# Four-layer graph network on one core: values of layers 1 and 2 by seven products, instructions moved off or merged on VectorE, and the first graph's adjacency codes turned by TensorE

## The chip, the core and the metric

The kernel runs on one core of one Trainium2 chip. TensorE (PE) multiplies, VectorE (DVE) and ScalarE (ACT) work element by element, GpSimd (POOL) and SyncE (SP) do little but issue transfers. Each engine works through its own list in order. The metric is the device time of one execution in microseconds (us), the median of several runs; lower is better.

## The reference

32 graphs (B) of 512 nodes (N) with 256 features (H) pass four attention layers, each with a layer norm and a ReLU ahead and a residual sum behind. All values are float32; the adjacency is an int32 matrix of 0 and 1.

```python
# x: (32, 512, 256), adj: (32, 512, 512)
h = relu(layernorm(x))                      # layer 0: two convolutions with one softmax
att = softmax(h @ att_W @ h^T / sqrt(256) + where(adj == 1, 0, -1000))
y = tanh(att @ (h @ W0 + b0)); y = tanh(att @ (y @ W1 + b1))
x = x + y
h = relu(layernorm(x))                      # layer 1
Wh = h @ W^T;  e = leaky(Wh@a1 + (Wh@a2)^T);  x = x + softmax(where(adj > 0, e, -9e15)) @ Wh
h = relu(layernorm(x))                      # layer 2
Hh = h @ W; e = where(adj, exp(-leaky(Hh@s + (Hh@d)^T)), 0); x = x + elu(e @ Hh / rowsum(e))
h = relu(layernorm(x))                      # layer 3
g = h @ W; e = leaky((g@a_1)^T + g@a_2 + g@a_12@g^T)
x = x + elu(h @ W_1 + (softmax(where(adj > 0, e, -9e15)) @ h) @ W_2)
```

## The kernel before

**Tiling.** The graphs are independent. One graph's nodes are four tiles of 128 partitions (NT = 4), its features two chunks of 128 (HC = 2). A matrix of scores is kept turned, as four chunks `e(l, c)` of 128x512 float32. A float32 product stands in the trace as two records of a matmul (a turn by TensorE as one).

**Order of the work.** The function `graph` (L461) writes nothing; it registers operations with an engine, a cost and what they come after. A planner (`Plan`, L53 to L202) then orders all operations of all 32 graphs: a list schedule with due times `APART` and `APART_LAST` (L64) apart, for which it tries several spacings, and margins `SLACK` (L67) on the costs. The instructions are issued in that one order (L1131), so each engine's list is fixed when the kernel is built, and several graphs are woven into each other on every engine. Memory comes from pools: 34 large pages, 8 PSUM banks, 5 buffers for values, `FLIGHT` = 5 graphs between their first and their last operation (L243).

**One layer.** `normed` (L521) makes statistics on VectorE (L526, L527), the root on GpSimd (L533), the normed tile on ScalarE (L540), and turns it: VectorE splits the float32 tile into two 16-bit planes (L545), a DMA on SP's queue turns them (L548), ScalarE joins them to `hT` (L560). The very first graph's first layer is turned by TensorE instead (L553).

**Seven products.** `seven` (L586) makes a product of 2x2 blocks with seven block products in place of eight. `block_sums` (L618) forms four sums of blocks on VectorE (L633), four instructions. The products alternate between two PSUM banks p and q: product 1 goes to p; its block is written out (`write`); products 6, 7 and 4 are then added to the same bank p, and after each the bank is read out by another `write`; products 2, 5 and 3 go to q, and `add` reads them into three of the blocks. So product 6 waits for the first `write`, 7 for the second, 4 for the third. Layer 0's features (L742), values (L768) and scores (L833) and layer 3's (L742, L768, L1006) are made so.

**Values of layers 1 and 2.** `scored_values` (L649) makes them without the seven: for each of four tiles two products of 128x128 by 128x258 (L658, the two extra columns are the scores' halves), and a copy by ScalarE (L662). `attend` (L711) multiplies the exponentials with the values (L721): 257 columns in layers 0 to 2, 259 in layer 3.

**Scores of layer 0.** `write_q` (L844) copies the bank by ScalarE (L847, three of the four blocks; L841 takes the exponential of the fourth straight from PSUM); `add_q` (L849) adds on VectorE (L850) and takes the exponential on ScalarE (L841); `masked0` (L856) multiplies each block with a mask on VectorE (L516 makes the mask from `codeT`).

**Adjacency.** `classes` (L505) turns two tiles of the int32 adjacency into bfloat16 codes, four DMA transposes on SP's queue (L508) turn them into `codeT`.

Of the kernel before, what the change touches and what calls it, by code (L numbers as in the profile page):

```python
# [13 lines left out]
BF16 = mybir.dt.bfloat16  # L14
# [11 lines left out]
LEAST = 2.0**-126  # L26
LOWEST = -3.0e38
# [25 lines left out]
class Plan:  # L53
# [10 lines left out]
    APART, APART_LAST = [1000.0 * k for k in range(32, 64, 2)], [1000.0 * k for k in (2, 8)]  # L64
    HOP = 100.0
    LAND, RATE = 2000.0, 200.0
    SLACK = {"V": (1.05, 0.0), "A": (1.05, 0.0), "G": (1.5, 0.0), "D": (1.0, 800.0)}  # L67
# [138 lines left out]
def kernel(  # L206
# [36 lines left out]
    FLIGHT = 5  # L243
    PAGES, VALUES = 34, 5
    TURNED = 2
    LEAD = 2
# [66 lines left out]
    make_identity(nc, ident)  # L313
    mhalf = const.tile([P, NT], F32, tag="mhalf", name="mhalf")
# [37 lines left out]

    def transposed(w_sb, dst, after, *keys):
        done = []
        for c in range(HC):
            key = f"bank{next(banks)}"

            def turn(c, key):
                for r in range(HC):
                    nc.tensor.transpose(W[key][:, r * P : (r + 1) * P], w_sb()[:, r, c * P : (c + 1) * P], ident)  # L360

            def out_of(c, key):
                nc.vector.tensor_copy(dst()[:, c, :], W[key][:, : HC * P])

            a = prepare("PE", pe(nt=HC), after, partial(turn, c, key), key, *keys)
            done.append(prepare("V", V_ADD, [a], partial(out_of, c, key), key, *keys))
        return done
# [41 lines left out]
    l1_aug, l2_aug = (tile_of(n, H + 2) for n in ("l1_aug", "l2_aug"))  # L409
# [5 lines left out]
    for n, dst, w, key in (("w0", w0_s, w0, "raw9"), ("att", att_s, att_w, "raw10")):  # L415
# [9 lines left out]
    l3_wide = raw("raw8", H + 2)  # L425
    a = [load(l1_sb, rows_of(l1_w), "raw0")]
    ready["l1"] = transposed(l1_sb, lambda: l1_aug[:, :, 2:], a, "raw0")
    a += [load_column(l1_ac, l1_a.rearrange("n o -> (n o)"))]
    ready["l1"] += product(lambda d: l1_aug[:, d, 0:2], l1_sb,
                           lambda c: l1_ac.rearrange("p (o c) -> p c o", o=2)[:, c, :], 2, a, "raw0")  # L430
    a = [load(l2_aug[:, :, 2:], rows_of(l2_w))]
    a = ready["l2"] = a + transposed(lambda: l2_aug[:, :, 2:], l2_wt, a, "raw1")
    a = a + [load_column(l2_ac, l2_a.rearrange("o n -> (o n)"))]
    ready["l2"] = a + product(lambda d: l2_aug[:, d, 0:2], l2_wt,
                              lambda c: l2_ac.rearrange("p (o c) -> p c o", o=2)[:, c, :], 2, a, "raw1")
# [25 lines left out]
    def graph(b, adj_before, x_before):  # L461
# [47 lines left out]

        coded, code = [], None  # L510
        for g in range(NT // 2):
            code = op("V", V_CODE, [got_adj[2 * g + 2], code], partial(classes, g), "adj", "code", "slot")
            coded += [op("D", D_TURN, [code], partial(turn_code, t), "code", "codeT") for t in (2 * g, 2 * g + 1)]

        def mask0():
            nc.vector.tensor_scalar(T["mask0"], T["codeT"], HUGE, TINY, ALU.is_equal, ALU.max)  # L516
# [4 lines left out]
        def normed(l, xs):  # L521
# [21 lines left out]
            def split(t):  # L543
                bits = T[f"xn{l}"][:, t, :].bitcast(U16).rearrange("p (h b) -> p b h", b=2)
                nc.vector.tensor_copy(T[f"planes{l}_{t}"], bits)  # L545
# [18 lines left out]
            for g in range(NT // 2):  # L564
# [7 lines left out]
                for t in (2 * g, 2 * g + 1):  # L572
# [8 lines left out]
                    a = op("V", V_SPLIT, [a], partial(split, t), f"xn{l}", flat)  # L581
# [36 lines left out]
        def block_sums(dst, source, b, after, left):  # L618
# [16 lines left out]
            one = op("V", V_SUM, after, partial(form, 1), dst, source)  # L635
            three = op("V", V_SUM, after, partial(form, 3), dst, source)
# [12 lines left out]
        def scored_values(l, hs, w_aug, ready):  # L649

            cols = w_aug.shape[2]
            vs = []
            for t in range(NT):
                key = f"bank_v{l}{t}"

                def product(t, key):
                    for c in range(HC):
                        nc.tensor.matmul(T[key][:, :cols], T[f"hT{l}"][:, c, t * P : (t + 1) * P],  # L658
                                         w_aug[:, c, :], start=(c == 0), stop=(c == HC - 1))

                def values(t, key):
                    nc.scalar.copy(T[f"v{l}"][:, t, :cols], T[key][:, :cols])  # L662

                a = op("PE", pe(n258=4), [hs[t]] + ready, partial(product, t, key), key, f"hT{l}")
                vs.append(op("A", A_HALF, [a], partial(values, t, key), key, f"v{l}"))
            return vs

        def leaky_exp_t(l, vs, sign):
# [24 lines left out]
            def leaky(c):  # L693
                row = T[key] if turned else T[key][:, 0, :]
                nc.scalar.activation(e(l, c), row, AF.Prelu, bias=T[v][:, c, 1:2], alpha=ALPHA)  # L695
# [15 lines left out]
        def attend(l, es, vs, use):  # L711
# [3 lines left out]
            lead = LEAD if l < 3 else 0  # L715
# [12 lines left out]
            return done  # L728

# [80 lines left out]
        else:  # L810
# [29 lines left out]
            def exp0(i, l, key=None):  # L840
                nc.scalar.activation(block_e0(i, l), two_tiles(key, 0, N // 2) if key else block_e0(i, l), AF.Exp,  # L841
                                     scale=float(H) ** -0.5)

            def write_q(i, l, key, start, after):  # L844
                if (i, l) == (1, 0):
                    return op("A", A_COPY, after, partial(exp0, i, l, key), key, f"e0_{l}")
                return op("A", A_COPY, after, lambda: nc.scalar.copy(block_e0(i, l), two_tiles(key, 0, N // 2)), key, f"e0_{l}")  # L847

            def add_q(i, l, key, start, after):  # L849
                a = op("V", V_MASK, after, lambda: nc.vector.tensor_tensor(  # L850
                    block_e0(i, l), block_e0(i, l), two_tiles(key, 0, N // 2), ALU.add), key, f"e0_{l}")
                exps.append(op("A", A_EXP, [a], partial(exp0, i, l), f"e0_{l}"))
                return exps[-1]

            def masked0(i, l):
                nc.vector.tensor_tensor(block_e0(i, l), block_e0(i, l), T["mask0"][:, two(l), half(i)], ALU.mult)  # L856

            exps = []
            qb = seven("q0", pe(n256=4), lambda x, right_after=right_after, left_after=left_after: right_after(x) + left_after(x),
                       ("hT0", "hs0", "fa0", "fs0"), partial(scores0, right, left), write_q, add_q)  # L860
            es = {il: op("V", V_MASK, [a, m0], partial(masked0, *il), "mask0", f"e0_{il[1]}") for il, a in qb.items()}
# [27 lines left out]
        for g in range(NT // 2):  # L889
# [16 lines left out]
            def add_z(t):  # L906
                nc.vector.tensor_add(T["x"][:, t, :], T["x"][:, t, :], T["z0"][:, t, :])
# [4 lines left out]
            xs += [op("V", V_ADD, [a], partial(add_z, 2 * g + j), "z0", "x") for j in range(2)]  # L912
# [6 lines left out]
        vs = scored_values(1, hs, l1_aug, ready["l1"])  # L919
# [3 lines left out]
        def second(t, a, key):  # L923
            def sums():
                nc.vector.reciprocal(T["rs1"][:, t : t + 1], T[key][:, H : H + 1])

            def add():
                xt = T["x"][:, t, :]
                nc.vector.scalar_tensor_tensor(xt, T[key][:, :H], T["rs1"][:, t : t + 1], xt, ALU.mult, ALU.add)
# [8 lines left out]
        vs = scored_values(2, hs, l2_aug, ready["l2"])  # L938
# [7 lines left out]
        def third(t, a, key):  # L946
            def sums():
                rs = T["rs2"][:, t : t + 1]

                nc.vector.tensor_scalar(rs, T[key][:, H : H + 1], LEAST, None, ALU.max)  # L950
# [3 lines left out]
            def lower():  # L954
                nc.scalar.activation(T["y2"][:, t, :], T[key][:, :H], AF.Exp, scale=T["rs2"][:, t : t + 1])

            def upper():
                nc.scalar.activation(T["r2"][:, t, :], T[key][:, :H], AF.Relu, scale=T["rs2"][:, t : t + 1])

            def add_lower():  # L960
                xt = T["x"][:, t, :]
                nc.vector.scalar_tensor_tensor(xt, T["y2"][:, t, :], 1.0, xt, ALU.min, ALU.add)

            def add_upper():
                xt = T["x"][:, t, :]
                nc.vector.scalar_tensor_tensor(xt, T["r2"][:, t, :], -1.0, xt, ALU.add, ALU.add)

            a = op("V", V_TWO, [a], sums, key)
            l = op("A", A_TANH, [a], lower, key, "y2")
            u = op("A", A_TANH, [a], upper, key, "r2")  # L970
            l = op("V", V_ADD, [l], add_lower, "y2", "x")
            return op("V", V_ADD, [l, u], add_upper, "r2", "x")

        xs = attend(2, es, vs, third)


# [12 lines left out]
        def block_v(i, l):  # L989
            return T["v3"][:, two(l), i * (HALF + 1) : (i + 1) * (HALF + 1)]  # L990

        def write_v(i, l, key, start, after):
            return op("A", A_HALF, after, lambda: nc.scalar.copy(block_v(i, l), two_tiles(key, start, HALF + 1)), key, "v3")

        def add_v(i, l, key, start, after):
            return op("V", V_SUM, after, lambda: nc.vector.tensor_tensor(
                block_v(i, l), block_v(i, l), two_tiles(key, start, HALF + 1), ALU.add), key, "v3")

        vb = seven("v3", pe(nt=4), lambda x: right_after(x) + ready["l3"], ("hT3", "hs3"), partial(by_nodes, l3_aug, right), write_v, add_v)
# [84 lines left out]
        def fourth(t, a, key):  # L1084
# [3 lines left out]
            def both_terms():  # L1088
                p = T[key][:, : H + LEAD].rearrange("p (i k) -> p i k", i=2)[:, :, :HALF]
# [77 lines left out]
```

## Time and profile before

| | us |
|---|---|
| median of three runs (2368.14, 2368.44, 2372.44) | 2368.44 |
| the profiled execution, device time | 2372.2 |
| its span in the trace | 2370.4 |
| busy: PE / PEld (weight loads) / DVE / ACT / POOL | 2347.1 / 1985.5 / 2029.9 / 1724.8 / 253.1 |

How to read it: a row of groups names line, engine, operation, what is written from what and how often, then the busy time in us, the mean duration of one in ns, and the idle time of the engine ahead of them with what ended it. The duration of one record includes a tail that overlaps the next: what an instruction costs an engine that is full is the time from its begin to the next one's begin, read from the timeline. The chain of waits follows the last instruction back to what released it. A row of the waits is: who waited, for whom, us in all, how often, the longest. In a table by stretches each engine's busy time has its number of records behind it, then come the granted TensorE clock (PEclk), the DMA share and GB/s.

### The profile page before, as it was taken

What the parts mean: (1) busy time and instruction counts of PE and PEld (TensorE: products, weight loads), DVE (VectorE), ACT (ScalarE), POOL (GpSimd) and SP (SyncE); (2) the same over time, 40 slices, a digit from 0 to 9 for tenths busy, and PEclk for the clock granted to TensorE, in tenths of its full rate; (3) what the DMA queues carried; (4) which work ended last, traced back from release to release, by engine and by line L of the source; (5) the groups of instructions that cost most, each with busy time, mean ns of one, the idle gap of its engine ahead of it and who ended that gap; (6) DMA issues with size and microseconds to landing.
All of it is one profiled execution on the core that took longest, in us unless ns stands there. A gap on an engine that the chain in (4) does not pass through costs nothing.

```text
span 2370.4 us, 36184 instructions
## 1 busy us (share of the span) xinstructions
PE 2347.1 (99%) x11590; PEld 1985.5 (84%) x11590; DVE 2029.9 (86%) x6042; ACT 1724.8 (73%) x3386; POOL 253.1 (11%) x315
## 2 busy tenths in 40 slices
PE   7999999999999999999999999999999999999999
PEld 5788888888888888888888888888888888888888
DVE  6777888889888898888898888988888888888789
ACT  5577777777777777777777777777777777766785
POOL 3000100011100111101110001110011100101110
PEclk9999999999999999999999999999999999999999
DMA  7421332433333433324333234333243332422221
GB/s 189 92 54 35 86 74 67 88 81 72 79 67 79 94 64 82 72 68 92 75 76 78 66 82 89 67 81 70 70 94 67 81 81 67 99 49 50 47 49 44
DMA packets 432015, 178.71 MB, mean 75 GB/s; under 512 B 386288, under 2 KB 403824, under 8 KB 431824
## 3 DMA queue, kind: packets, MB, share of 16 engines
q1 hardware_dynamic: 426464, 158.03, 31.0%
q0 software_dynamic: 5216, 18.23, 2.3%
q8 instruction: 92, 1.51, 0.3%
q14 instruction: 99, 0.81, 0.1%
q10 hardware_dynamic: 144, 0.13, 0.0%
HBM read 67.64 MB, written 16.89 MB: 36 GB/s over the span
## 4 chain that ended last, share of the span: by engine, by line
PE 94%; DVE 3%; DMA 1%; ACT 1%; issue 0%; POOL 0%; SPq 0%; DVEq 0%; ACTq 0%; POOLq 0%
PE bank_a L721 36%; PE bank_z L878 9%; PE bank_v L658 9%; PE bank_o L896 5%; PE bank_s3p L1006 4%; PE bank_q0p L833 4%; PE bank_f3p L742 4%; PE bank_v0p L768 4%; PE bank_w3p L768 4%; PE bank_f0p L742 4%; PE bank_s3q L1006 3%; PE bank_q0q L833 3%; PE bank_v3p L768 2%; PE bank_v3q L768 2%; DMA planesT<-planes 1%; DVE st L526 0%
## 5 line engine op out<-in xcount | busy, mean ns | idle before, releaser
L721 PE MATMUL bank_a<-v,e 128*128 128x257 f32 (+1 forms) x4096 | 986.2, 381 | 5.1 <-DVE e L808 3.2
L721 PEld LDWEIGHTS bank_a<-v,e 128*128 128x128 f32 x4096 | 769.4, 190 | 164.6 <-issue 53.9
L560 ACT COPY hT<-planesT 128x512 uint16<-128x512 uint16 x508 | 378.2, 767 | 43.7 <-DMA planesT<-planes 43.3
L533 POOL TENSOR_TENSOR rstd<-ve,mhalf 128x2 f32<-128x2 f32 x256 | 218.3, 883 | 1668.7 <-DVE ve L530 1142.9
L540 ACT ACTIVATE xn<-x,off,rstd 128x256 f32<-128x256 f32 x512 | 276.2, 594 | 40.6 <-DVE off L536 39.8
L658 PE MATMUL bank_v<-l_aug,hT 128*128 128x258 f32 x1024 | 257.1, 381 | 1.0 <-ACT hT L560 0.8
L878 PE MATMUL bank_z<-e,y 128*128 128x512 f32 x512 | 240.6, 592 | 0.0
L545 DVE COPY planes<-xn 128x512 uint16<-128x512 uint16 x508 | 204.7, 416 | 20.6 <-DMA planesT<-planes 15.3
L658 PEld LDWEIGHTS bank_v<-l_aug,hT 128*128 128x128 f32 x1024 | 191.2, 190 | 28.4 <-ACT hT L560 1.4
L526 DVE BATCH_NORM_STATS2 st<-x 128x6 f32<-128x256 f32 x512 | 208.6, 407 | 4.3 <-DMA x<-in_x_dram 4.2
L1052 ACT ACTIVATE e<-e,zero 128x512 f32<-128x512 f32 x128 | 88.1, 717 | 96.5 <-DVE crest L1030 95.0
L695 ACT ACTIVATE e<-row,v 128x512 f32<-128x512 f32 x224 | 153.0, 715 | 4.5 <-DMA row<-row 4.3
L698 ACT ACTIVATE e<-e 128x512 f32<-128x512 f32 x256 | 156.2, 629 | 0.0
L662 ACT COPY v<-bank_v 128x258 f32<-128x258 f32 x256 | 95.9, 375 | 81.5 <-PE bank_v L658 79.8
L878 PEld LDWEIGHTS bank_z<-e,y 128*128 128x128 f32 x512 | 97.0, 190 | 68.0 <-issue 57.6
L869 ACT ACTIVATE y<-bank_a,rs 128x256 f32<-128x256 f32 x128 | 56.8, 470 | 83.0 <-DVE rs L866 83.0
L1013 DVE SCALAR_TENSOR_TENSOR e<-bank_s3p,v,mask 128x256 f32<-128x256 f32 x256 | 111.1, 475 | 6.5 <-PE bank_s3p L1006 6.3
L896 PE MATMUL bank_o<-w_sb,zT 128*128 128x256 f32 x512 | 116.1, 379 | 0.0
L896 PEld LDWEIGHTS bank_o<-w_sb,zT 128*128 128x128 f32 x512 | 97.0, 190 | 13.2
L527 DVE BATCH_NORM_AGGREGATE mv<-st 128x2 f32<-128x6 f32 x512 | 93.1, 182 | 17.5
L841 ACT ACTIVATE e<-e 128x512 f32<-128x512 f32 x93 | 58.5, 629 | 56.8 <-DVE e L850 56.8
L1058 ACT ACTIVATE e<-e 128x512 f32<-128x512 f32 x128 | 76.8, 634 | 18.5 <-DVE e L1055 18.5
(186 smaller groups left out, 4361.9 us busy)
## 6 DMA issues: line engine op xcount, KB each, us to landing
adj<-in_adj_dram SPq DMA_DIRECT2D x128, 256.0 KB, 2.9
x<-in_x_dram SPq DMA_DIRECT2D x31, 512.0 KB, 5.1
out_dram<-y POOLq DMA_DIRECT2D x31, 512.0 KB, 4.1
row<-row SPq DMA_DIRECT2D x56, 256.0 KB, 3.5
planesT<-planes SPq DMA_TRANSPOSE x508, 2.4
codeT<-code SPq DMA_TRANSPOSE x128, 2.5
crest<-crest SPq DMA_TRANSPOSE x64, 2.4
row<-sT SPq DMA_DIRECT2D x56, 2.0 KB
```

The lines of the kernel that those rows point to most:

```text
L526: nc.vector.bn_stats(T[f"st{l}"][:, t, :], T["x"][:, t, :])
L533: nc.gpsimd.tensor_tensor(T[f"rstd{l}"][:, two(g)], T[f"ve{l}"][:, two(g)], mhalf[:, two(g)], ALU.pow)
L540: nc.scalar.activation(T[f"xn{l}"][:, t, :], T["x"][:, t, :], AF.Relu, bias=T[f"off{l}"][:, t : t + 1], scale=T[f"rstd{l}"][:, t : t + 1])
L545: nc.vector.tensor_copy(T[f"planes{l}_{t}"], bits)
L560: nc.scalar.copy(bits[:, :, :, t * P : (t + 1) * P], T[f"planesT{l}_{t}"].rearrange("p (b c) n -> p b c n", b=2))
L658: nc.tensor.matmul(T[key][:, :cols], T[f"hT{l}"][:, c, t * P : (t + 1) * P], w_aug[:, c, :], start=(c == 0), stop=(c == HC - 1))
L721: nc.tensor.matmul(T[key][:, : LEAD + H + 1 - lead], e(l, c)[:, t * P : (t + 1) * P], T[f"v{l}"][:, c, lead:], start=(c == 0), stop=(c == ...
L742: nc.tensor.matmul(p[:, : N // 2], w[:, x - 1, :], right(x), start=fresh, stop=True, skip_group_check=True)
L768: nc.tensor.matmul(p[:, j * k : (j + 1) * k], right(x)[:, j * P : (j + 1) * P], w[:, x - 1, :], start=fresh and j == 0, stop=True, skip_gr ...
L833: nc.tensor.matmul(p[:, j * N // 2 : (j + 1) * N // 2], right(x)[:, j * P : (j + 1) * P], left(x), start=fresh and j == 0, stop=True, skip ...
L878: nc.tensor.matmul(T[f"bank_z{k}"], T["y0"][:, c, k * P : (k + 1) * P], e(0, c), start=(c == 0), stop=(c == NT - 1))
L896: nc.tensor.matmul(T[key][:, j * H : (j + 1) * H], T["zT"][:, k, t * P : (t + 1) * P], w1_sb[:, k, :], start=(k == 0), stop=(k == HC - 1))
```

## The change

- Layers 1 and 2: the values are made by `seven`, with `scored_values` now shared with layer 3. A product is 128x128 by 128x129; two of them for each of seven blocks. Four sums of blocks are formed per layer, three blocks get an `add` on VectorE. The weights are laid out and combined once at the start. The values' score columns move, and `attend` takes 258 columns in these layers in place of 257.
- `block_sums` on the side of `hT`: two of the four sums in one instruction, three instructions in all.
- Layer 0's scores: `write_q` is now an addition of bank and mask on VectorE for all four blocks; the mask holds 0 or -1104 in place of 1 or 0; ScalarE's copies and VectorE's multiplications with the mask are gone, and all four exponentials are taken in place. The first graph keeps its old way.
- Layer 1: the split into planes is ScalarE's (`BYACT`).
- Sums into `x` of layers 0 and 2 take two tiles in one instruction.
- First graph: codes turned by TensorE (16 turns of 128x128 in bfloat16) and copied from PSUM by VectorE, in place of four DMA transposes.
- The planner: `FLIGHT` 6 in place of 5, margins 1.03 in place of 1.05 on VectorE and ScalarE, two more spacings to try at the end.

```diff
-    APART, APART_LAST = [1000.0 * k for k in range(32, 64, 2)], [1000.0 * k for k in (2, 8)]
+    APART, APART_LAST = [1000.0 * k for k in range(32, 64, 2)], [1000.0 * k for k in (2, 5, 8, 12)]
-    SLACK = {"V": (1.05, 0.0), "A": (1.05, 0.0), "G": (1.5, 0.0), "D": (1.0, 800.0)}
+    SLACK = {"V": (1.03, 0.0), "A": (1.03, 0.0), "G": (1.5, 0.0), "D": (1.0, 800.0)}
-    FLIGHT = 5
+    FLIGHT = 6
+    BYACT = (1,)
...
+        def turn_code_pe(t, key):
+            for c in range(NT):
+                nc.tensor.transpose(T[key].bitcast(BF16)[:, c * P : (c + 1) * P], T["code"][:, t, c * P : (c + 1) * P], ident16)
+        def code_of(t, key):
+            nc.vector.tensor_copy(T["codeT"][:, :, t * P : (t + 1) * P],
+                                  T[key].bitcast(BF16)[:, :N].rearrange("p (c n) -> p c n", c=NT))
...
-            coded += [op("D", D_TURN, [code], partial(turn_code, t), "code", "codeT") for t in (2 * g, 2 * g + 1)]
+            for t in (2 * g, 2 * g + 1):
+                if b:
+                    coded.append(op("D", D_TURN, [code], partial(turn_code, t), "code", "codeT"))
+                else:
+                    key = f"bank_c{t}"
+                    a = op("PE", pe(nt=NT), [code], partial(turn_code_pe, t, key), "code", key)
+                    coded.append(op("V", V_MASK, [a], partial(code_of, t, key), key, "codeT"))
...
-            nc.vector.tensor_scalar(T["mask0"], T["codeT"], HUGE, TINY, ALU.is_equal, ALU.max)
+            if b == 0:
+                nc.vector.tensor_scalar(T["mask0"], T["codeT"], HUGE, TINY, ALU.is_equal, ALU.max)
+            else:
+                nc.vector.tensor_scalar(T["mask0"], T["codeT"], HUGE, AWAY, ALU.not_equal, ALU.mult)
...
-                nc.vector.tensor_copy(T[f"planes{l}_{t}"], bits)
+                (nc.scalar.copy if l in BYACT else nc.vector.tensor_copy)(T[f"planes{l}_{t}"], bits)
...
+            def form_two():
+                nc.vector.tensor_tensor(T[dst][:, 0:3:2, :], T[source][:, :, half(1)],
+                                        T[source][:, 0, :].rearrange("p (l n) -> p l n", l=2), ALU.subtract)
+            if left:
+                one = op("V", V_SUM, after, partial(form, 1), dst, source)
+                three = op("V", V_SUM, after, partial(form, 3), dst, source)
+            else:
+                one = three = op("V", V_MASK, after, form_two, dst, source)
...
-        def scored_values(l, hs, w_aug, ready):
...
-                        nc.tensor.matmul(T[key][:, :cols], T[f"hT{l}"][:, c, t * P : (t + 1) * P],
-                                         w_aug[:, c, :], start=(c == 0), stop=(c == HC - 1))
...
+        def scored_values(l, after, right, w, ready):
+            def block(i, l_):
+                return T[f"v{l}"][:, two(l_), i * (HALF + 1) : (i + 1) * (HALF + 1)]
+            def write(i, l_, key, start, after):
+                return op("A", A_HALF, after, lambda: nc.scalar.copy(block(i, l_), two_tiles(key, start, HALF + 1)),
+                          key, f"v{l}")
+            def add(i, l_, key, start, after):
+                return op("V", V_SUM, after, lambda: nc.vector.tensor_tensor(
+                    block(i, l_), block(i, l_), two_tiles(key, start, HALF + 1), ALU.add), key, f"v{l}")
+            return seven(f"v{l}", pe(nt=4), lambda x: after(x) + ready, (f"hT{l}", f"hs{l}"), partial(by_nodes, w, right),
+                         write, add)
...
-            lead = LEAD if l < 3 else 0
+            lead = (LEAD, 1, 1, 0)[l]
...
             def write_q(i, l, key, start, after):
+                a = op("V", V_MASK, after + [m0], lambda: nc.vector.tensor_tensor(
+                    block_e0(i, l), two_tiles(key, 0, N // 2), T["mask0"][:, two(l), half(i)], ALU.add),
+                    key, f"e0_{l}", "mask0")
                 if (i, l) == (1, 0):
-                    return op("A", A_COPY, after, partial(exp0, i, l, key), key, f"e0_{l}")
-                return op("A", A_COPY, after, lambda: nc.scalar.copy(block_e0(i, l), two_tiles(key, 0, N // 2)), key, f"e0_{l}")
+                    return op("A", A_EXP, [a], partial(exp0, i, l), f"e0_{l}")
+                return a
...
-            def masked0(i, l):
-                nc.vector.tensor_tensor(block_e0(i, l), block_e0(i, l), T["mask0"][:, two(l), half(i)], ALU.mult)
...
-            def add_z(t):
-                nc.vector.tensor_add(T["x"][:, t, :], T["x"][:, t, :], T["z0"][:, t, :])
+            def add_z(g):
+                nc.vector.tensor_add(T["x"][:, two(g), :], T["x"][:, two(g), :], T["z0"][:, two(g), :])
...
-        vs = scored_values(1, hs, l1_aug, ready["l1"])
+        right_after, right = block_sums("hs1", "hT1", lambda j, l: T["hT1"][:, j, half(l)], hs, left=False)
+        vb = scored_values(1, right_after, right, l1_aug, ready["l1"])
+        vs = [tuple(vb.values())] * NT
...
-            def add_lower():
-                xt = T["x"][:, t, :]
-                nc.vector.scalar_tensor_tensor(xt, T["y2"][:, t, :], 1.0, xt, ALU.min, ALU.add)
+        def add_lower(g):
+            xt = T["x"][:, two(g), :]
+            nc.vector.scalar_tensor_tensor(xt, T["y2"][:, two(g), :], 1.0, xt, ALU.min, ALU.add)
```

Layer 2 and the second half of layer 2's residual (`add_upper`) change in the same way as the lines shown.

## The prediction, made before the changed kernel ran

> **What bounds the kernel now.** I read the page's busy shares and its chain of waits first, then who waits on PE, then the stretches, then timelines for what one instruction costs. Page:
>
> ```profile
> PE 2347.1 (99%) x11590; PEld 1985.5 (84%) x11590; DVE 2029.9 (86%) x6042; ACT 1724.8 (73%) x3386; POOL 253.1 (11%) x315
> PE 94%; DVE 3%; DMA 1%; ACT 1%; issue 0%; POOL 0%; SPq 0%; DVEq 0%; ACTq 0%; POOLq 0%
> ```
>
> PE is busy almost throughout, and 94% of the chain that ends last is PE. A busy PE need not be a full one, so I look at PE's waits over the whole span, and after them at the stretch from 200 to 2000 us, which answers with a single row:
>
> ```profile
> PE bank_n L553 <- ACT xn L540: 9.3, 1, 9.3
> PE bank_a L721 <- DVE e L808: 3.2, 1, 3.2
> PE bank_q0p L833 <- ACT e L847: 1.2, 2, 0.9
> ```
>
> ```profile
> PE bank_v L658 <- ACT hT L560: 0.6, 1, 0.6
> ```
>
> In 1800 us PE waited 0.6 us. There the time is the sum of PE's records, about 72.6 us for a graph (layer 0's second convolution recurs at 575.51, 648.24 and 720.84 us in the chain). Whatever shortens PE's list shortens the span by as much, as long as the others keep up. The stretches tell how far they are from not keeping up (a middle one, the begin, the end):
>
> ```profile
> 1200.00:1600.00 400.00, 400.00 (x1958) 338.23 (x1957) 351.12 (x1048) 296.26 (x581) 44.32 (x51) 1.00 0.35 77
> ...
> 32.00:36.00 4.00, 4.00 (x12) 3.25 (x13) 3.28 (x10) 1.70 (x3) 1.52 (x2) 0.62 1.06 262
> ...
> 2275.00:2310.00 35.00, 33.23 (x185) 28.77 (x185) 33.93 (x120) 32.64 (x71) 6.14 (x7) 1.00 0.25 54
> ```
>
> Middle: DVE 88%, ACT 74%. Begin: the granted clock is 0.62 just after a PE wait. End: DVE is 97% busy and PE no longer full.
>
> What a record costs a full PE is the step from begin to begin; likewise on DVE:
>
> ```profile
> 1031.62 0.61 PE L768 MATMUL bank_w3p<-l_w1s,hT 128*128 128x128 f32 x4
> 1032.06 1.04 PE L658 MATMUL bank_v<-l_aug,hT 128*128 128x258 f32 x4
> 1032.93 0.59 PE L742 MATMUL bank_f3p<-hs,m 128*128 128x256 f32 x2
> ...
> 1049.13 0.61 PE L768 MATMUL bank_v3q<-l_aug,hs 128*128 128x129 f32 x4
> 1049.58 1.03 PE L1006 MATMUL bank_s3q<-hT,fa 128*128 128x256 f32 x4
> ```
>
> ```profile
> 1006.97 0.42 DVE L633 TENSOR_TENSOR hs<-hT 128x256 f32<-128x256 f32 x1
> 1007.31 0.15 DVE L536 SCALAR_TENSOR_TENSOR off<-mv,rstd 128x2 f32<-128x2 f32 x1
> 1007.38 0.68 DVE L1055 TENSOR_TENSOR e<-e,crest 128x512 f32<-128x512 f32 x1
> 1007.98 0.42 DVE L633 TENSOR_TENSOR hs<-hT,hs 128x256 f32<-128x256 f32 x1
> ```
>
> Four records of 258 columns take 0.87 us, four of 129 columns 0.44 to 0.45 us. On DVE 256 elements take 0.34 us, 512 take 0.60 us: merging two saves 0.08 us.
>
> **The change, part by part.**
>
> *PE, the values.* Before: 2 layers x 32 graphs x 4 tiles x 2 products x 2 records = 1024 records, 256 fours of 0.87 = 222.7 us. After: 2 x 32 x 7 x 2 x 2 = 1792 records, 448 fours of 0.445 = 199.4 us. **-23.3 us** (-25.6 with 0.44, -21.1 with 0.45). Layer 3's values run in exactly this shape now. Against it: attention of layers 1 and 2 takes one column more, 2048 records x 0.87/4/258 us = **+1.7 us**.
>
> [...]
>
> *PE, the codes.* 16 turns in bfloat16 are added; no bfloat16 record is in the trace. Below: nothing. Above: a float32 record of 128 columns, 0.11 us, so 1.8 us. I take that nearest row: **+1.8 us**.
>
> *The start.* PE idles 3.2 us until the mask is multiplied in (L808), because the mask waited 2.5 us for the four DMA turns of the codes; the eight records after it then take 3.40 us to the next begin (31.80 to 35.20) where eight take 1.74 elsewhere, at a low clock: 1.7 us. With PE turning the codes, the DMAs go (SP's queue held them for 5.2 us ahead of graph 1's own turns). What is late next, by the changed lists: the second code stands behind two more pairs of statistics (0.53 each), so it ends near 21.3 us; one sum and one split (0.34 each), four copies and other rows bring the mask to about 25.7 us and the first two products with it to 27.4 us, while PE, with 1.8 us of turns, is at the scores until 28.5 us (the weights' turns that it did next, from 26.7 us, come later at the same cost). So the wait goes and with it the low clock: **-4.9 us**. If the mask is late by more than 1 us it returns in part: bounds -6 and 0.
>
> [...]
>
> *DVE, per graph.* Added in each of two layers: one sum of 512 (0.60), two of 256 (0.34), three additions from PSUM (0.34): 2.30, together 4.6 us. Gone: four splits (1.36); merged sums into x, six merges of pairs in the sums into x (0.48), two merges of block sums in layers 0 and 3 (0.16): 2.0 us. Layer 0's scores stay: three additions and four masks become seven additions. Net +2.6 us. DVE goes from 63.7 us (351.12/400 x 72.6) to 66.3 of 71.9: 92%. ACT gets four splits (at most L560's 767 ns) and loses three copies (L847, 584 ns): +1.3 us on 53.8, 77%. Both hide under PE in the middle, so I cost them **nothing** there; without that cover they cost what PE then waits (first rival).
>
> *The end.* The order is remade, so I count both lists. From the last graph's second convolution to its first attention product of layer 2, DVE's list before holds 54.7 us of begins for 61.3 us of PE's; after, 95.0 for 96.1. DVE is as good as full there, and every wait for PE or ACT is then lost. From there to the end both are alike (81.6 for 85.9; 81.8 for 84.6). Below nothing. Above 9 us: DVE idled 6.6 of the 61.3 us before; the same share of 96.1 us is 10.4, and 1.1 are free. I take the nearest row: from 2275 to 2310 us, with DVE 97% busy, PE stood 1.8 of 35 us; over 96 us that is 4.9, and PE already lost 0.9 in this stretch before (61.06 of 62 us busy from 2213 to 2275): **+4 us**.
>
> *At no cost:* combining two more weights (12 short DVE instructions) and one more load on POOL, in a start where DVE is 74% busy (44.52 of the 60 us after 40). FLIGHT, margins and spacings issue nothing; they make the order. In the lists a middle graph now spans 390 us of PE's work instead of 312, and from layer 0's second convolution to layer 1's values lie 37 us of other work instead of 20, the one place where the middle waited.
>
> *Sum* on the profiled span: 2370.4 - 23.3 + 1.7 + 1.8 - 4.9 + 4.0 = 2349.7 us; with the 1.8 us around it (2372.2 - 2370.4) 2351.5. The median of the runs is 3.8 us lower than that execution, which gives 2347.7: **2348 us**. Of the three runs one was as long as the profiled one, so up to 2352 is still this case.
>
> **Rivals.**
>
> *A new wait on DVE takes the gain (slower, 0.11).* Layer 0's score bank p was freed by ACT (74% busy); now DVE frees it, three times a graph before the next product may start. In the changed lists of graph 15, PE has 1.74 us of other work between the first and second of these products, where it had 4.35. DVE has about 4.1 us of work between the last feature addition and this read, PE 3.9 until the bank is full; with its 0.68 us the read ends some 0.75 us before PE needs the bank. Late by more than that, PE pays the rest in each graph: the gain of 20.7 us is gone when DVE is 0.75 + 0.65 us late each time, and at 2.2 us late the wait is 32 x 1.45 = 46 us, that is 2394 us. For it: DVE at 92%, in order. Against it: PE never waited for DVE between 200 and 2000 us, though DVE frees the value bank of layer 0 in the same way (L818).
>
> *Part of the gain stays in start and end (0.15).* The mask late, DVE short in the last 180 us: 5 to 15 us more, 2356 to 2363.
>
> *It does not do what it says (0.07).* The 129-column products, set among others, do not run at half the time; at 0.50 us for four the values save nothing, and the rest cancels: 2364 to 2373. Against it the rows above.
>
> *More comes (0.05).* 0.44 us for four, turns free, end at no cost: 2370.4 - 25.6 + 1.7 - 6 + 1.8 = 2342, less the 3.8 of the median 2338 or below.
>
> **How the numbers follow.** The forecast (2340 to 2356) has 0.62. With the second rival and halves of the two on either side the range 2339 to 2364 holds about 8 in 10. A measurement of this kernel tells 0.2% (4.7 us) from no change: faster 0.62 + 0.15 + 0.05 = 0.82, same 0.07, slower 0.11.
>
> **What would show it.** Right: L768's shape of 129 columns about 1792 records richer at 0.44 us for four, L658 gone; no PE wait on the mask at the start and clock 1.00 from 26 to 36 us; a middle stretch of 400 us still with under 1 us of PE waits and DVE at 90 to 93%; a graph every 71.9 us. Wrong: rows of PE waiting for DVE's score additions in the middle, or a graph's step that stays at 72.6 us with PE below 99%.

## The result, and the profile after

The changed kernel takes **2353.43 us** (median of four runs, 2352.92 to 2354.90) against 2368.29 us of the kernel before (2367.40 to 2372.44): a ratio of 0.9933, 95% interval 0.9921 to 0.9946, or 14.9 us less. The forecast was 2348 us, with a range from 2339 to 2364: faster as forecast, and 5.4 us above the number. The profiled execution of the changed kernel is the longest of the four, 2354.9 us with a span of 2353.1.

The page of the changed kernel, busy shares and chain:

```profile
PE 2328.9 (99%) x12374; PEld 1992.0 (85%) x12374; DVE 2099.7 (89%) x6060; ACT 1719.9 (73%) x3421; POOL 254.2 (11%) x316
PE 94%; DVE 4%; DMA 1%; ACT 1%; issue 0%; POOL 0%; DVEq 0%; ACTq 0%
```

PE still sets the time. It has 784 records more and is busy 18.2 us less. Who waits on PE over the whole span of the changed kernel:

```profile
PE bank_n L584 <- ACT xn L571: 8.8, 1, 8.8
PE bank_f3p L783 <- ACT fa L793: 2.0, 1, 2.0
PE bank_w3p L809 <- ACT w L1108: 1.9, 1, 1.9
PE bank_q0p L874 <- DVE e L885: 1.5, 3, 0.6
PE bank_a L758 <- DVE e L956: 0.9, 1, 0.9
```

The wait of 3.2 us for the mask is gone. Two waits of 2 us for ACT are new. The stretches of the changed kernel tell where they lie:

```profile
26.00:32.00 6.00, 6.00 (x31) 4.99 (x30) 5.51 (x18) 3.82 (x8) 2.70 (x5) 1.00 1.01 277
32.00:36.00 4.00, 4.00 (x17) 2.78 (x16) 3.62 (x18) 2.69 (x6) 2.66 (x4) 1.00 0.70 46
...
1200.00:1600.00 400.00, 399.86 (x2141) 344.92 (x2140) 363.31 (x1050) 291.66 (x582) 44.15 (x51) 1.00 0.35 76
2250.00:2280.00 30.00, 26.06 (x124) 21.93 (x123) 28.30 (x94) 27.72 (x59) 5.07 (x6) 0.94 0.21 40
2275.00:2310.00 35.00, 35.00 (x203) 31.89 (x203) 33.65 (x92) 22.33 (x47) 2.67 (x3) 0.98 0.23 47
```

The same stretch of 30 us near the end, before the change:

```profile
2250.00:2280.00 30.00, 28.59 (x140) 23.92 (x139) 24.02 (x73) 23.66 (x49) 3.39 (x4) 1.00 0.17 33
```

From 26 to 36 us PE is now full at clock 1.00 (it was 0.62 from 32 us on). The middle is as full as it was. From 2250 to 2280 us PE stands for 3.9 of 30 us where it stood for 1.4, DVE and ACT are 94% and 92% busy instead of 80% and 79%, and the clock is 0.94.

**Where the 17.3 us of span went.** Waits show only a part of what PE loses. So I gave every PE record a usual step from begin to begin (about 1 ns and 0.838 ns a column, at least 0.1112 us; 0.056 us for a turn in bfloat16), summed them as PE's list, and counted by how much each begin comes later than that. The steps are read from the traces: the median is 0.112 us for 129 columns, 0.216 us for 256 and 0.429 us for 512. All rows are worked out from the traces in this way (us):

| | before | after |
|---|---|---|
| PE's list at usual steps | 2333.4 | 2313.0 |
| ahead of the first record | 9.3 | 8.8 |
| lost from 0 to 100 us | 10.4 | 5.5 |
| lost from 100 to 2000 us | 5.3 | 6.7 |
| lost from 2000 us to the last record | 6.1 | 12.1 |
| from the last record's begin to the end | 6.0 | 6.9 |
| span | 2370.4 | 2353.1 |

PE's list brings 20.4 (21.3 without the 0.9 of the turns), the start 5.4; the middle costs 1.4 and the end 6.9.

### The profile page after: what moved, and what is told of

Its sections match the earlier page's. It is cut to its first block, busy times and chain, and to the rows that moved or that the text cites. A ratio compares the mean times of both kernels' runs of the same rounds, so it can differ in the third digit from the quotient of the medians.

```text
span 2353.1 us, 37623 instructions
## 1 busy us (share of the span) xinstructions
PE 2328.9 (99%) x12374; PEld 1992.0 (85%) x12374; DVE 2099.7 (89%) x6060; ACT 1719.9 (73%) x3421; POOL 254.2 (11%) x316
## 4 chain that ended last, share of the span: by engine, by line
PE 94%; DVE 4%; DMA 1%; ACT 1%; issue 0%; POOL 0%; DVEq 0%; ACTq 0%
PE bank_a L758 36%; PE bank_z L918 9%; PE bank_s3p L1040 5%; PE bank_o L936 4%; PE bank_q0p L874 4%; PE bank_f3p L783 4%; PE bank_w3p L809 4%; PE bank_v0p L809 4%; PE bank_f0p L783 4%; PE bank_s3q L1040 3%; PE bank_q0q L874 3%; PE bank_v1p L809 2%; PE bank_v3p L809 2%; PE bank_v2p L809 2%; PE bank_v3q L809 2%; PE bank_v1q L809 2%
## 5 line engine op out<-in xcount | busy, mean ns | idle before, releaser
L758 PE MATMUL bank_a<-v,e 128*128 128x258 f32 (+2 forms) x4096 | 1017.7, 381 | 0.9 <-DVE e L956 0.9
L758 PEld LDWEIGHTS bank_a<-v,e 128*128 128x128 f32 x4096 | 744.1, 190 | 108.9 <-issue 18.2
L576 DVE COPY planes<-xn 128x512 uint16<-128x512 uint16 x380 | 156.4, 420 | 17.3 <-DMA planesT<-planes 10.2
L882 ACT ACTIVATE e<-e 128x512 f32<-128x512 f32 x124 | 77.8, 629 | 121.9 <-DVE e L893 61.8
L735 ACT ACTIVATE e<-e 128x512 f32<-128x512 f32 x256 | 157.1, 630 | 0.0
L695 ACT COPY v<-bank_v1p 128x258 f32<-128x258 f32 x128 | 47.7, 373 | 120.0 <-PE bank_v1p L809 119.3
L936 PEld LDWEIGHTS bank_o<-w_sb,zT 128*128 128x128 f32 x512 | 95.8, 190 | 12.8 <-ACT zT L922 0.6
L664 DVE TENSOR_TENSOR hs<-hT,hs 128x256 f32<-128x256 f32 x254 | 105.1, 414 | 1.1
L667 DVE TENSOR_TENSOR hs<-hT 128x512 f32<-128x512 f32 x127 | 86.6, 682 | 14.5 <-ACT hT L591 14.3
L885 DVE TENSOR_TENSOR e<-bank_q0p,mask 128x512 f32<-128x512 f32 x124 | 84.5, 682 | 13.8 <-PE bank_q0p L874 12.3
L1089 DVE TENSOR_TENSOR e<-e,crest 128x512 f32<-128x512 f32 x128 | 85.9, 682 | 8.3 <-ACT crest L1083 8.1
```

The source lines that it names most:

```text
L735: nc.scalar.activation(e(l, c), e(l, c), AF.Exp, scale=sign)
L758: nc.tensor.matmul(T[key][:, : LEAD + H + 1 - lead], e(l, c)[:, t * P : (t + 1) * P], T[f"v{l}"][:, c, lead:], start=(c == 0), stop=(c == ...
L936: nc.tensor.matmul(T[key][:, j * H : (j + 1) * H], T["zT"][:, k, t * P : (t + 1) * P], w1_sb[:, k, :], start=(k == 0), stop=(k == HC - 1))
```

## The experiments

"Lost" below is counted in the same way. Every ratio is to the kernel before on the same chip, whose median there was 2369.05, 2369.96 or 2370.41 us. So a difference of some 2 us between medians from two chips can be the chips'.

### The seven products without the relief of DVE

Edit of the changed kernel: `BYACT` empty, layer 0's scores copied by ACT and multiplied with the mask on DVE, sums not merged.

```diff
-    BYACT = (1,)
+    BYACT = ()
...
-            a = op("V", V_MASK, after + [m0], lambda: nc.vector.tensor_tensor(
-                block_e0(i, l), two_tiles(key, 0, N // 2), T["mask0"][:, two(l), half(i)], ALU.add),
+            return op("A", A_COPY, after, lambda: nc.scalar.copy(block_e0(i, l), two_tiles(key, 0, N // 2)), key, f"e0_{l}")
```

> The changed kernel with its relief of VectorE undone: layer 1's split on VectorE again, layer 0's scores copied by ScalarE and multiplied with the mask on VectorE, sums into x and block sums unmerged. PE's list is that of the changed kernel, VectorE's about 2 us a graph longer, ScalarE's 1.3 us shorter. Theory (PE's list sets the time, VectorE only loses something at the ends): 2354 to 2366 us, few PE waits from 200 to 2000 us. Rival (the relief is what lets the seven products pay): VectorE at 94 to 95% makes PE wait in every graph, 2368 us or more.

Measured: 2374.38 us (2371.07 to 2378.80), ratio 1.0019 (1.0011 to 1.0028). The time lies in the rival's range: the whole gain is gone. Its mechanism is not seen, though: DVE is 92% busy, not 94 to 95%, and from 200 to 2000 us PE has 7 waits of 5.0 us in all, not one in every graph. Its middle:

```profile
1200.00:1600.00 400.00, 398.61 (x2134) 343.69 (x2133) 367.54 (x1114) 285.23 (x573) 43.71 (x50) 1.00 0.35 75
```

PE's list is that of the changed kernel, 2313.0 us. From 100 to 2000 us it loses 19.5 us instead of 6.7, most of it in small pieces, and after 2000 us 17.6 instead of 12.1. But an engine that is 92% busy instead of 91% is a thin cause for this, so the same instructions were put in another order:

```diff
-    SLACK = {"V": (1.03, 0.0), "A": (1.03, 0.0), ...
+    SLACK = {"V": (1.02, 0.0), "A": (1.02, 0.0), ...
```

> The seven products without the relief of DVE, as in the run that took 2374 us (layer 1's split on DVE, layer 0's scores copied by ACT and multiplied with the mask on DVE, no merged sums), with margins of 1.02 instead of 1.03: the same instructions as in that run, ordered by a planner that counts DVE and ACT a little cheaper. Theory (DVE itself has no room without the relief, so another order doesn't help): 2366 to 2380 us, PE 398 to 399.5 us busy of 400 in the middle. Rival (that run lost by its order, and the relief is worth little): 2351 to 2360 us, PE full in the middle.

Measured: 2361.35 us (2358.69 to 2362.23), ratio 0.9963 (0.9950 to 0.9977). Between the two: neither held. The middle is nearly full again, with DVE at 93% (it loses 2.8 us from 1200 to 1600 us; the run above 4.0, the changed kernel 1.2):

```profile
1200.00:1600.00 400.00, 399.44 (x2142) 343.69 (x2141) 370.31 (x1124) 288.21 (x576) 41.58 (x51) 1.00 0.35 75
```

So 13 of the 21 us that the lack of relief seemed to cost were the order, not DVE. What is left for the relief is some 8 us, between two kernels with different margins.

### The seven products taken out, twice

Layers 1 and 2 get their values by eight block products again, in 1024 records of 258 columns; relief, turns and planner stay.

```diff
-        vb = scored_values(1, right_after, right, l1_aug, ready["l1"])
-        vs = [tuple(vb.values())] * NT
+        vs = plain_values(1, hs, l1_aug, ready["l1"])
```

> The changed kernel, but the values of layers 1 and 2 are made tile by tile with 258 columns as before; the relief of VectorE, the codes on PE and the planner's settings stay. Theory (in the middle the relief is worth nothing, PE is full): 21.6 us more of PE's list, so 2368 - 6 at the start and at most 3 less at the end: 2359 to 2364 us, a graph every 72.6 us. Rival (the relief itself is the gain): 2350 to 2356 us.

Measured: 2380.48 us (2380.01 to 2381.41), ratio 1.0046 (1.0032 to 1.0059): slower than before, and both expectations missed. PE's list is 2334.3 us, 21.3 more than with the seven products; by the counts of records at their usual steps that term of the prediction (-23.3 + 1.7 = -21.6) holds. Of what is lost besides, 6.0 us lie here:

```profile
200.00:400.00 200.00, 196.02 (x938) 163.52 (x937) 155.50 (x459) 142.45 (x285) 20.80 (x25) 1.00 0.32 67
```

DVE is only 78% busy, and PE stands nevertheless. That looks like an order that has no work ready and not like a lack of an engine. To test it, the same kernel with `FLIGHT = 5`:

> The changed kernel with the values of layers 1 and 2 made by eight block products in records of 258 columns (as in the run that took 2380 us), and with five graphs in flight instead of six; relief of DVE, turns by TensorE and margins of 1.03 stay. Theory (its 2380 us came from the order that six in flight give a list whose graphs don't need the sixth): 2360 to 2371 us, no slower than before. Rival (the relief itself, layer 0's score bank freed by DVE instead of ACT, costs PE something, and the seven products hide it): 2376 us or more, with PE waiting for DVE ahead of bank_q0p.

Measured: 2366.91 us (2366.19 to 2368.19), ratio 0.9989 (0.9980 to 0.9998), as the theory had it. PE loses 3.8 us from 100 to 2000 us, the least of all these kernels:

```profile
200.00:400.00 200.00, 200.00 (x983) 168.79 (x982) 167.48 (x485) 148.61 (x294) 22.29 (x26) 1.00 0.32 73
```

So the change without its seven products, in an order that suits it, is worth some 3 us, and adding the seven products with six in flight 13.5 us more, not 21: PE's list shrinks by 21.3, the span by 12.8, and the rest comes back as losses, 4.4 us of it after 2000 us and 2.9 in the middle.

### The planner's settings

The changed kernel with `FLIGHT` 5, margins 1.05 and end spacings of 2 and 8:

> The changed kernel with the planner's settings of before: 5 graphs in flight, margins 1.05, two spacings for the end. Theory (no instruction differs, the order only moves losses at the ends): 2351 to 2359 us. Rival (the longer chains need the sixth graph, else PE runs dry in the middle): 2365 us or more, with PE waits in every graph.

Measured: 2402.20 us (2398.71 to 2402.48), ratio 1.0134 (1.0120 to 1.0147). The time is the rival's, 37 us above its bound. Which of the three settings it is: the two added end spacings do nothing, since without them every engine's list comes out the same, instruction by instruction. The other two were tried alone.

```diff
-    FLIGHT = 6
+    FLIGHT = 5
```

> The changed kernel with five graphs in flight instead of six; margins of 1.03, the spacings, all instructions stay. Theory (the sixth graph is what the seven products live on: in the changed lists a graph lasts 390 us of PE's work, and five graphs at a step of 71.9 us allow 360): PE must wait for operations of a graph that isn't let in yet, as with the whole old planner, so 2395 to 2410 us, with 15 us or so lost from 200 to 400 us and 1 to 3 us in every 200 us after that. Rival (the margin of 1.03 instead of 1.05 carried the 48 us): within 5 us of the changed kernel, 2349 to 2358. Halfway, 2370 to 2385: both carry a part.

Measured: 2400.12 us (2399.20 to 2402.64), ratio 1.0130 (1.0116 to 1.0144). The stretch and the first waits on PE from 200 to 600 us of this kernel:

```profile
200.00:400.00 200.00, 194.63 (x1043) 166.23 (x1041) 181.00 (x528) 151.21 (x299) 22.59 (x27) 0.99 0.36 76
```

```profile
PE bank_a L758 <- DVE e L986: 2.1, 3, 0.8
PE bank_v2p L809 <- ACT v L695: 1.7, 2, 1.2
PE bank_v0p L809 <- DVE v L864: 1.6, 2, 1.4
PE bank_q0q L874 <- DVE e L893: 1.2, 2, 0.6
```

The time is as the theory had it. All kinds of products wait, each a little. PE loses 32.9 us from 100 to 2000 us, 10.5 of them from 200 to 400 us, and 31.1 after that. The other setting:

```diff
-    SLACK = {"V": (1.03, 0.0), "A": (1.03, 0.0), ...
+    SLACK = {"V": (1.05, 0.0), "A": (1.05, 0.0), ...
```

> The changed kernel with the planner's margins on VectorE's and ScalarE's costs at 1.05, as before the change, instead of 1.03; six graphs in flight, all instructions the same. Theory (the sixth graph carried the larger part of the 48 us that the old planner's settings cost, as the run with five in flight says, 2400 us; the margin is worth something of its own, because the planner that counts DVE 2% dearer takes it for full): 2360 to 2375 us, with the loss spread over the middle. Rival (beside the sixth graph the margin is nothing): 2350 to 2357 us.

Measured: 2370.34 us (2368.74 to 2372.64), ratio 1.0001 (0.9993 to 1.0010). The time is the theory's. Two hundredths of margin, in numbers that only the planner sees, are worth the whole gain too: 20.8 us are lost from 100 to 2000 us. They are not spread evenly: 8.8 lie between 150 and 200 us, where PE waits 2.7 us for DVE and then has half the clock for 6.8 us. The two settings don't add up (47 and 17 us alone, 49 together).

Is it then the settings and not the products? The kernel before with the new settings:

> The kernel before with the planner's settings of the changed one alone: six graphs in flight, margins of 1.03, four end spacings; every instruction is the old one. Theory (a graph of before lasts 312 us of PE's work, less than the 363 us that five graphs allow, so the sixth finds nothing to do, and PE was full in the middle anyway): 2364 to 2376 us, no change or a little slower. Rival (the room itself is a good part of the gain, whatever the products): 2360 us or less.

Measured: 2374.47 us (2371.57 to 2377.07), ratio 1.0017 (1.0008 to 1.0026), in the theory's range. The settings alone make the old kernel a little slower. They are needed by the new products and worth nothing without them. The reason given in these expectations doesn't hold, though. From the first code of a graph (L519 here, L505 before) to its last sum (L1137; L1103) lie 336 us before the change, 420 after, but 423 in the old kernel with six in flight as well: the planner fills what it is given, so a graph's stay doesn't tell how many it needs.

### Another order of the same instructions

> The changed kernel with the graphs' due times 33 thousand units apart instead of the 32 that the planner takes from its steps of two: the same instructions in another order on every engine. Theory (the sum of PE's records sets the time, the order only its rims): within 5 us of 2353.4, that is 2348 to 2358 us; the middle from 200 to 2000 us loses as little (about 6 us) and what differs lies in the first 100 and the last 200 us. Rival (the order decides as much as the instructions, and 2353 was a lucky one): 2365 us or more. If this one differs by 2 us or more, the 2.1 us between the changed kernel and the one with the codes turned by DMA say nothing on the codes.

Measured: 2353.15 us (2351.79 to 2356.60), ratio 0.9933 (0.9920 to 0.9945). As the theory had it: of these two neighbours neither was lucky. Only part of the difference lies where it was expected: 8.2 us are lost after 2000 us instead of 12.1, but 8.6 instead of 6.7 in the middle, and the first 100 us are as before.

### The codes by DMA again, in two orders

```diff
-                if b:
+                if True:
                     coded.append(op("D", D_TURN, [code], partial(turn_code, t), "code", "codeT"))
```

> The changed kernel, but the first graph's codes are turned by DMA again. Theory (the start gained about 6 us by the missing wait for the mask and the low clock after it): 2358 to 2361 us, with a PE wait of about 3 us on the mask near 30 us. Rival (the start's gain comes from the new order, or is filled with other work): 2352 to 2355 us.

Measured: 2355.52 us (2354.16 to 2356.27), ratio 0.9939 (0.9927 to 0.9951): 2.1 us above the changed kernel, between the two ranges. With the spacing of the section before this one:

> The changed kernel at the spacing of 33 thousand units (2353.2 us with the codes turned by TensorE), with the first graph's codes turned by DMA again. A second pair of orders for the same question. Theory (the turns by TensorE take away a wait of 3 us and a stretch at the low clock, 4.9 us by my sum): 2356 to 2359 us, with PE waiting for the mask near 26 us and a clock below 1.00 after it. Rival (the order fills that wait with something else, and 2 us or less are left of it, as in the first pair): 2351 to 2356 us.

Measured: 2354.57 us (2354.12 to 2356.35), ratio 0.9937 (0.9925 to 0.9950): 1.4 us above its partner, in the rival's range. The wait for the mask is there again in both kernels. In this second one it is 2.4 us, but no low clock follows, against the theory:

```profile
PE bank_a L758 <- DVE e L849: 2.4, 1, 2.4
```

```profile
26.00:32.00 6.00, 3.62 (x21) 2.69 (x20) 5.46 (x20) 3.46 (x7) 5.96 (x9) 1.00 0.99 219
32.00:36.00 4.00, 4.00 (x22) 3.55 (x21) 2.96 (x7) 1.14 (x2) 2.80 (x4) 1.00 1.13 226
```

In the first kernel, whose wait is 2.8 us, the low clock is there:

```profile
26.00:32.00 6.00, 3.21 (x17) 2.79 (x16) 5.45 (x16) 3.60 (x6) 5.98 (x9) 0.83 0.88 219
32.00:36.00 4.00, 4.00 (x19) 3.46 (x18) 2.32 (x7) 0.62 (x2) 0.32 (x1) 0.82 1.20 215
```

Where the codes are turned and waited for, from 20 to 40 us, the kernels with the codes by DMA lose 4.6 and 3.9 us, those with the turns by TensorE 0.05 each. Less the 0.9 of the turns themselves that is 3.7 and 2.9 us (the prediction's terms, -4.9 and +1.8, make 3.1). What is left of it at 100 us differs: in all they lose 8.0 and 10.5 us up to there, and 5.5 and 5.3 with the turns. That leaves 1.6 and 4.3 us: the first kernel gets 2 us back from 40 to 100 us, and the second loses 1 us more already before 20 us. In the medians 2.1 and 1.4 us arrive (by the ratios 1.4 and 0.9). The intervals overlap with those of their partners, so by the times alone the size is not settled.

### A better version

Layer 1's splits go back to DVE in the last three graphs, and the planner gets finer spacings, margins of 1.035 and an allowance `PASS` of 175 instead of 200.

```diff
-    PASS = 200.0
+    PASS = 175.0
-    APART, ... = [1000.0 * k for k in range(32, 64, 2)], ...
+    APART, ... = [1000.0 * k for k in range(26, 38, 1)], ...
-                (nc.scalar.copy if l in BYACT else nc.vector.tensor_copy)(T[f"planes{l}_{t}"], bits)
+                (nc.scalar.copy if l in BYACT and b < B - 3 else nc.vector.tensor_copy)(T[f"planes{l}_{t}"], bits)
```

> A try at a better version: the changed kernel with the splits of layer 1 back on DVE in the last three graphs (ACT, 92% busy from 2250 to 2280 us, was what PE waited for there), the planner's spacings tried in steps of one thousand units instead of two from 26 to 37, margins 1.035 and the allowance of 200 units behind every operation cut to 175. Theory (of the 12 us that PE loses after 2000 us a third to a half can be had back by the order and by less ACT): 2345 to 2351 us. Rival (what is given back at the end is lost elsewhere by another order, as between spacings 32 and 33, which differ by 0.3 us): 2351 to 2358 us.

Measured: **2348.18 us** (2348.00 to 2348.98), ratio 0.9910 (0.9896 to 0.9923): 5.3 us below the changed kernel, as the theory had it, with intervals of the ratio that just touch. Middle and end of this kernel:

```profile
1200.00:1600.00 400.00, 400.00 (x2146) 345.38 (x2146) 364.34 (x1055) 291.73 (x585) 42.91 (x52) 1.00 0.34 76
2250.00:2280.00 30.00, 28.00 (x142) 22.69 (x141) 29.16 (x96) 27.40 (x61) 5.32 (x5) 1.00 0.24 46
```

It loses 5.1 us in the middle instead of 6.7, and 8.6 after 2000 us instead of 12.1. In its middle layer 0's second convolution recurs every 71.9 us (71.5 to 72.5); in the changed kernel the steps go 71.9, 71.1, 71.9, 73.3 and again. How much of this is the split and how much the order was not separated.

## Why the prediction was right, and where it was off

**The values: right, mechanism and size.** Forecast -23.3 + 1.7 = -21.6. PE's list with and without the seven products differs by 21.3. A piece of the changed kernel's timeline:

```profile
1031.79 0.61 PE L809 MATMUL bank_v2q<-l_aug,hs 128*128 128x129 f32 x4
1032.24 0.60 PE L783 MATMUL bank_f0p<-hT,att_s 128*128 128x256 f32 x2
1032.67 0.61 PE L809 MATMUL bank_w3p<-l_w1s,hT 128*128 128x128 f32 x4
```

Four records of 129 columns, 0.45 us; there are 2688 such records now, where 896 were before. So they do run at half, and that rival falls. From the fifth to the 28th graph the step is 71.8 us on average (forecast 71.9). The 784 records more bring as many weight loads. Summed by their durations the loads take 2205 us of 2370 before (93%) and 2356 of 2353 after (100%); by the page's busy shares, in which overlapping loads count once, 84% and 85%. So 150 us of load time were added, and the kernel became 14.9 us shorter: the loads overlap, and their sum was no bound.

**The turns: half of what I took.** "I take that nearest row: +1.8 us." The turns of the changed kernel and what follows them:

```profile
20.69 1.06 PE L526 MATMUL bank_c<-ident,code 128*128 128x128 bf16 x16
21.58 5.37 PE L843 MATMUL bank_q<-fa,hT 128*128 128x512 f32 x12
26.79 1.03 PE L758 MATMUL bank_a<-v,e 128*128 128x257 f32 x4
```

16 turns take 0.89 us from begin to begin, 0.056 each. The scores after them run 5.21 us for 12 records, the usual 0.43 each, at clock 1.00. So these 0.89 us of turns cost nothing behind them.

**The start: right where it acts.** The wait on the mask and the low clock are gone, and the losses of the first 100 us fell by 4.9 us, with 0.5 more ahead of the first record: 5.4, for the forecast 4.9. From 20 to 40 us alone they fell from 5.0 to 0.05, and with the codes by DMA 4.6 and 3.9 us come back there. How much of that reaches the end is not settled: the medians change by 2.1 and 1.4 us, where my two terms make 3.1. Other waits take the mask's place: in the stretch from 40 to 60 us, which was full, PE now loses 3.0 us.

**DVE and ACT in the middle at nothing: the number held, the reason only in part.** From 1200 to 1600 us DVE is 90.8% busy (forecast 92), ACT 72.9% (forecast 77; its splits take 616 ns, for which I took the bound of 767), PE waits 0.9 us from 200 to 2000, and the middle loses 1.4 us more than before. The rival of a new wait on bank p did not come: PE waits for L885 1.5 us in the whole kernel. But the cover is not made by room on the engines. With DVE 93% busy and no relief, PE lost 2.8 us in the 400 us from 1200 to 1600; with DVE only 78% busy and no seven products, it lost 6.0 in the 200 us from 200 to 400.

**The step that was too weak: "FLIGHT, margins and spacings issue nothing; they make the order", at no cost.** True of the sum, and too little for a forecast. Five in flight costs 47 us, margins of 1.05 cost 17, on the very same instructions. My sum holds only for an order that keeps PE fed, and that it would be kept fed I had read from two details of the lists (a graph's stay, and the distance between two products), of which the stay is no measure. That the changed kernel came with settings that feed PE was luck as far as my sum goes. The kernel's own planner could have told: `replay` (L107) runs an order at the planner's costs. Computed from the kernels' sources alone it gives 2368.5 us before, 2350.7 after, 2402.1 with five in flight and 2369.0 with margins of 1.05, each within 3 us of the median. It is no sure guide either: for the seven products without the relief it gives 2358.2, and 2374.4 was measured.

**The end: mis-sized.** Forecast +4 with bounds of 0 and 9; measured +6.9. I looked to DVE, and at the place that costs most it was ACT's order. The chain in the changed kernel's timeline:

```profile
2270.60 1.59 ACT L571 ACTIVATE xn<-x,off,rstd 128x256 f32<-128x256 f32 x3
2272.09 0.47 ACT L793 ACTIVATE fa<-bank_f3p,l_u 128x256 f32<-128x256 f32 x1
...
2272.61 1.04 PE L783 MATMUL bank_f3p<-hT,m 128*128 128x256 f32 x2 [2.01 <-ACT fa L793]
2273.45 1.06 PE L783 MATMUL bank_f3p<-hs,m 128*128 128x256 f32 x2
2274.30 1.06 PE L809 MATMUL bank_w3p<-l_w1s,hT 128*128 128x128 f32 x4
```

Three normed tiles stand just ahead of the read of bank f3p on ACT, which is busy without a gap, and PE waits for that read for 2.0 us. Then the steps of two records double: 0.84 and 0.85 us instead of 0.43. With the wait of 1.9 us for w (L1108) six us earlier, this place makes 6.1 us, half of all that is lost after 2000 us.

**The sum.** By the span: forecast -20.7, measured -17.3. The terms are off by +0.3 (values and attention), -0.9 (turns), -0.5 (start), +1.4 (middle) and +2.9 (end): +3.2, and 0.2 of rounding. The other 2 us of the 5.4 come from the profiled executions: that of before was 3.8 us above its median, which I took off, that of after only 1.5.

## What to carry to other kernels

Where one engine's list sets the time, the sum of its begin-to-begin steps tells what a change of its records is worth, and a change that lengthens no other list beyond it can still lose all of that in the order: try the planner's settings anew with each change, both for the new version and for the one that leaves a part out. An ablation under settings that were chosen for the whole overstates the part: here 21 us in place of 8 for the relief, 27 in place of 13.5 for the products. Whether a kernel is as good as its sum is read from the losses by stretch, and those at the rims, more than the middle, were what an even better order could still take back (3.5 us against 1.6).

## What was not expected of the hardware

A low clock came after a wait of PE of 2.0 us, and not after one of 1.9 us six us earlier, nor after one of 2.4 us in another kernel. The clock in the changed kernel, stretch by stretch (the waits of 1.9 and 2.0 us end at 2266.6 and 2272.6 us):

```profile
2266.50:2269.50 3.00, 2.91 (x16) 2.56 (x17) 2.90 (x13) 2.41 (x6) 1.69 (x2) 1.00 0.31 60
2269.50:2272.50 3.00, 1.09 (x7) 0.82 (x6) 3.00 (x8) 3.00 (x8) 0.00 (x0) 1.00 0.00 0
2272.50:2275.00 2.50, 2.39 (x8) 2.04 (x8) 2.50 (x8) 2.09 (x7) 0.00 (x0) 0.57 0.27 52
2275.00:2278.00 3.00, 3.00 (x15) 2.65 (x15) 2.86 (x12) 2.98 (x8) 0.00 (x0) 0.79 0.24 46
2278.00:2281.00 3.00, 3.00 (x18) 2.66 (x17) 2.63 (x10) 2.27 (x6) 1.88 (x2) 1.00 0.41 80
```

After the first wait the clock stayed at 1.00. After the second it was 0.50 from 2272.83 to 2276.24 us (two of the rows mix this with 1.00), and the five groups from 2272.61 to 2276.61 us took 4.00 us where such groups take 2.2. A wait of 2 us thus cost nearly twice its length.

The length of a single wait does not decide it in these runs. A low clock followed the wait of 2.0 us here, that of 2.8 us in the kernel with the codes by DMA (0.83 from 26 to 32 us and 0.82 from 32 to 36 us) and that of 3.2 us in the kernel before (0.50 from 31.62 to 35.03 us). After the wait of 2.4 us in the kernel with the codes by DMA at the spacing of 33 the clock stayed at 1.00 from 26 to 36 us. The low stretch held for 3.41 us both here and in the kernel before. What else decides it was not shown.

A turn in bfloat16 began 0.056 us after the one before, half of the 0.111 us of a float32 record with the same columns.
